# Neighbour keys made on VectorE in bf16, and attention products for two gathers at once with ScalarE copying the sums

## The chip, the cores and the metric

The kernel runs on one core of a Trainium2 chip. The metric is device time in microseconds (us) of one execution, and a kernel's time is the median over several runs. The core's engines run at the same time, each through its own stream of instructions in order: TensorE (PE; its weight loads are listed as PEld), VectorE (DVE), ScalarE (ACT), GpSimd (POOL) and SyncE (SP). Transfers to and from main memory are issued by an engine's queue and run beside it.

## The reference

Two layers over 4096 nodes with 128 features. The graph is a random 0/1 matrix `adj` with density 1/128, so a node has some 32 neighbours (a list has room for 64). Layer 0 is graph attention with eight heads, layer 1 takes three quantiles over the neighbours that a rule keeps.

```python
# layer 0, cut
Wh = jnp.einsum('nd,hde->hne', nodes, W)
f1 = jnp.einsum('hnd,hd->hn', Wh, a1)
f2 = jnp.einsum('hnd,hd->hn', Wh, a2)
e = leaky_relu(f1[:, :, None] + f2[:, None, :], 0.2)
att = softmax(where(adj > 0, e, -9e15))
h = elu(jnp.einsum('hnm,hmd->hnd', att, Wh))
x = elu(cat(h) @ W1 + b1)
x = layernorm(nodes + x, gamma, beta)
# layer 1, cut
svals = sort(where(keep, x[neighbours], big))
agg = mean over q in (0.25, 0.5, 0.75) of svals[ceil(q * n_keep) - 1]
out = (0.5 * agg + 0.5 * x) @ W.T + b + x
```

## The kernel before

No dense attention matrix is made. Each tile of 128 nodes is first searched for the list of its neighbours; then a gather fetches, for each place of the list, the row of that neighbour; and the softmax-weighted sum of the rows is taken before the product with W (the sum over neighbours and the product with W change places).

**Search** (`neighbours`, L535 to L589). The adjacency of a tile comes in two halves of 128x2048 int32, loaded from ScalarE's queue (L544, three buffers). ScalarE makes it `sgn`, 0 or 1 in bf16, and counts it (L550, two buffers). Per piece of 512 columns TensorE makes search keys in PSUM: 8192 times sgn (L571, lhsT `markb`) plus a falling count of columns from `parts` (L573). VectorE takes the eight largest of each 128 columns (L577, four `max8` per piece) into `first`, 128x256. After the second half, eight rounds of `max8` and `match_replace` (L584, L586) give the 64 largest in order, and L589 takes the 8192 off again, so that a list holds falling positions, padded with zeros. `neighbours` yields after each piece and each pair of rounds, so others can be placed between.

**Blocks.** Tiles go in blocks of 2, 8 and 22 (L377 to L417). The nodes of a block are ranked by their number of neighbours (`rank_by_count`) and scattered in that order, so that tile i of a block needs only lists up to a cap, from 24 to 63 places. The first 2 tiles are searched at the start, the next 8 while the first block is attended, the next 22 while the second is. In these two blocks `tc.manual_schedule` keeps the order of the written program on VectorE, TensorE and ScalarE (`ORDERED`, L410). In the last block, with no search left, a scheduler orders the instructions.

**One step** (`step`, L345 to L375) fetches tile i, weighs tile i-1 and transforms an earlier group of tiles. `fetch_rows` (L755 to L813) loads the lists on SP's queue, transposes them (L786) and the scores f1 (L794, L799), and issues the indirect gathers on GpSimd (L185). One gather brings 128 rows: 32 places of the lists of four nodes in a part of width 32, which has 32 gathers for the 128 nodes, or 16, 8 or 4 places of 8, 16 or 32 nodes in parts of that width, which have as many gathers as places. So a tile with cap 35 has parts of 32 and 4 and takes 36 gathers. A part of 32 fills a buffer G, a short rest goes into Gs (16 gathers); both have two buffers, and G a third in the last block. `weigh_rows` (L816 to L901) is cut by yields, between which the step takes a turn of the transform and `each` pieces of the search.

**Weighing.** For each part: z = exp(leaky_relu(f1 + f2)) (L829 and L830 on VectorE, L831 on ScalarE); pf, 128x1024, which spreads z onto the right nodes (L835); then TensorE sums G's rows over the partitions with columns of pf as weights into y (L847), one matmul for each gather, or two or more where its nodes and heads pass 128 columns. The result has a row for each node and head of the gather (4 x 8 = 32 rows in a full part) and 129 columns: 128 features and a one, for the denominator. y is three PSUM banks with one buffer and holds 8 blocks of 128x129. So in a full part four matmuls fill the rows of one block. After the last part VectorE takes the denominators (L868, L875) and normalises out of PSUM (L879). TensorE transposes (L896) and ScalarE copies yT (L897).

**Transform** (`transform`, L904 to L988) does, for two tiles (four in the last block), the products with W (L939, into hT), the exp of the elu (L947), the elu (L917, L919), the product with W1 (L925), a second elu (L952 to L956), and the layer norm (L966 to L986), whose rows a GpSimd scatter writes to x1 (L194, called x_d in the trace). hT comes from the pool `pp` in the first two blocks and from the key pool `kp` in the last.

**Quantiles.** The rest gathers rows of x1 (L185, named vals) and sorts them in a network of minima and maxima on VectorE (L1145), with copies by ScalarE (L1141).

Of the kernel before, what the change touches and what calls it, by code (L numbers as in the profile page):

```python
# [23 lines left out]
H = 8  # L24
# [9 lines left out]
MARK = 8192.0  # L34
# [30 lines left out]
TURN = 12  # L65

# [142 lines left out]
def kernel(  # L209
# [97 lines left out]
    parts = adjp.tile([64, N], BF16, name="parts", bufs=1)  # L307
    markb = adjp.tile([P, P], BF16, name="markb", bufs=1)
    nc.vector.memset(oneb, 1.0)
    nc.vector.tensor_scalar(markb, ident, MARK, None, ALU.mult)  # L310

    nc.gpsimd.memset(parts, 0.0)
    iota(nc, parts[0:1, :], [[-64, N // 64], [0, 64]], base=N)
    iota(nc, parts[32:33, :], [[0, N // 64], [-1, 64]])
# [4 lines left out]
    def search(t0, n):  # L319
        return neighbours(  # L320
            tc, adjp, kp, rec, num, adj, range(t0, t0 + n), parts, markb, oneb
        )
# [22 lines left out]
    def step(fetch=None, pieces=None, quota=0, size=2, more=None):  # L345
# [5 lines left out]
        if len(weigh) > 1 or (weigh and not fetch):  # L351
# [3 lines left out]
            turns = sum(2 + -(-w // 8) for w, *_ in parts) + 3  # L355
# [9 lines left out]
            if len(members) == size:  # L365
                tails.append(
                    transform(tc, attp, pp, more or pp, turned.pop(0), list(members), consts, store)
                )
                members.clear()
# [8 lines left out]
    for b, n in enumerate(BLOCKS):  # L378
# [28 lines left out]
        else:  # L407
            pieces = search(t0 + n, BLOCKS[b + 1])
            quota = -(-BLOCKS[b + 1] * PIECES // n)
            with tc.manual_schedule(engines=ORDERED):  # L410
                for i in range(n):
                    step((recs_d[b], i, CAPS[n][i], t0 + i), pieces, quota)
# [122 lines left out]
def neighbours(tc, adjp, kp, rec, num, adj, tiles, parts, markb, oneb):  # L535
# [24 lines left out]
    while signs:  # L560
# [7 lines left out]
        for b in range(half // 512):  # L568

            key = kp.tile([P, 512], F32, name="key")  # L570
            nc.tensor.matmul(key, lhsT=markb, rhs=sgn[:, ts(b, 512)], start=True, stop=False)  # L571
            c0 = i * half + b * 512
            nc.tensor.matmul(  # L573
                key, lhsT=oneb[0:64, :], rhs=parts[:, c0 : c0 + 512], start=False, stop=True
            )
            for c in range(512 // CW):
                nc.vector.max(first[:, ts(c0 // CW + c, 8)], key[:, ts(c, CW)])  # L577
# [3 lines left out]
        nc.vector.tensor_tensor(num[:, t : t + 1], cnt[:, 0:1], cnt[:, 1:2], ALU.add)  # L581
        for r in range(L // 8):
# [6 lines left out]
        nc.vector.tensor_scalar(rec[:, t, 0:L], rec[:, t, 0:L], -MARK, 0.0, ALU.add, ALU.max)  # L589
# [165 lines left out]
def fetch_rows(tc, ap, narrow, rec_d, i, cap, t, xt_d, bad, turn):  # L755
# [26 lines left out]
    for s0, w in layers(cap):  # L782
# [22 lines left out]
        elif s0 % 32 == 0:  # L805

            few = sum(v for s, v in layers(cap) if s >= s0) <= 16
            G, col = take(ap, [P, 16 if few else 32, XW], "Gs" if few else "G", turn), 0
# [7 lines left out]
def weigh_rows(tc, ap, pools, pp, parts, turned, place, size, consts):  # L816
# [5 lines left out]
    y = pp.tile([P, 3, 512], F32, name="y")  # L822

    def block(b):
        return y[:, b // 3, (b % 3) * (D + 1) : (b % 3 + 1) * (D + 1)]

# [568 lines left out]
```

## The time and the profile before

| what | value |
|---|---|
| median of 6 runs | 4426.52 us (4419.93 to 4429.68) |
| profiled execution | 4424.82 us |
| span of it | 4423.1 us |
| mean granted TensorE clock | 0.558 |
| busy: PE, PEld | 979.5 us (22%), 516.9 us (12%) |
| busy: VectorE | 2532.4 us (57%) |
| busy: ScalarE | 1029.0 us (23%) |
| busy: GpSimd | 2296.4 us (52%) |
| gathers G of attention | 1092, mean 972 ns |

By time, the span falls into: start, with the search of two tiles (0 to 95 us); the first block, with the search of eight (95 to 320); the second block, with the search of 22 (322 to 1110); ranking and scattering (1110 to 1180); the last block (1180 to 2380, with a tail to 2444); the quantiles (2444 to 4423). Each stage has its own busy engine, so the shares over the whole span say little about one of them.

A line of the waits names the engine and line that waited, what released it, and then microseconds in total, number of times and the longest. "remote" is a releaser that can't be named from the records, and "issue" is time in which the engine waited for nothing that the profile shows. In lists of groups, x stands ahead of a count, then come busy microseconds and mean nanoseconds of one, and after the second bar the idle time ahead.

### The profile page before, as it was taken

To read this page: it belongs to the slowest core of one execution; us is meant where nothing else is said; L and a number is where in the kernel's file an instruction comes from. 1 tells how busy PE (TensorE), PEld (TensorE's weight loads), DVE (VectorE), ACT (ScalarE), POOL (GpSimd) and SP (SyncE) were. 2 spreads that over 40 slices of the span, in tenths; PEclk is the share of its full clock that TensorE was granted. 3 is DMA by queue.
4 is the path that set the end of the run, shared out by engine and by line. 5 is a ranking of instruction groups with operands and counts; after the bars stand their busy time and mean duration, and the time that the engine had idled before them with its cause. 6 is when DMAs were issued, how large, how long until landed. Compare 5 with 4: busy or idle time off the path is not lost. (4 is left out here: it accounts for less than half of the span.)

```text
span 4423.1 us, 19775 instructions
## 1 busy us (share of the span) xinstructions
PE 979.5 (22%) x4289; PEld 516.9 (12%) x4289; DVE 2532.4 (57%) x4862; ACT 1029.0 (23%) x1424; POOL 2296.4 (52%) x2453
## 2 busy tenths in 40 slices
PE   4323444443222233233233000000000001000101
PEld 2001211111111111121122000000000000000001
DVE  5554556555321124111121437888878999999898
ACT  2101212111000011000010213333333444434333
POOL 2433443344567666757564675666575334455530
PEclk9955555556556555555565555555555555555555
DMA  5313323221121121212111111111111001111100
GB/s 169 107 48 113 99 91 107 88 93 43 48 49 50 47 56 44 58 41 56 44 49 32 48 52 39 48 45 48 35 50 36 23 21 33 31 36 36 38 28 3
DMA packets 115233, 241.26 MB, mean 55 GB/s; under 512 B 51904, under 2 KB 68288, under 8 KB 106912
## 3 DMA queue, kind: packets, MB, share of 16 engines
q0 software_dynamic: 76224, 161.01, 13.2%
q10 hardware_dynamic: 12160, 68.49, 4.4%
q1 hardware_dynamic: 26720, 10.41, 1.1%
q14 instruction: 93, 0.76, 0.1%
q8 instruction: 36, 0.59, 0.1%
HBM read 228.56 MB, written 11.18 MB: 54 GB/s over the span
## 5 line engine op out<-in xcount | busy, mean ns | idle before, releaser
L1145 DVE TENSOR_TENSOR vals<-low,vals 128x1024 f32<-128x1024 f32 (+9 forms) x1359 | 1402.2, 1057 | 333.6 <-ACT low L1141 116.1
L185 POOL DMA_INDIRECT G<-xt_d,idx x1092 | 1061.0, 972 | 730.5 <-issue 400.2
L185 POOL DMA_INDIRECT vals<-x_d,idx x960 | 911.0, 949 | 296.0 <-issue 283.5
L1141 ACT COPY low<-vals 128x1024 f32<-128x1024 f32 (+10 forms) x701 | 607.2, 876 | 971.6 <-DVE vals L1145 662.7
L1155 PE MATMUL st_ps<-ident,u 128*128 128x128 f32 x344 | 86.2, 433 | 1776.4 <-ACT u L1154 1346.4
L577 DVE MAX8 first<-key 128x8 f32<-128x128 f32 x1024 | 223.7, 283 | 346.4 <-remote 230.7
L194 POOL DMA_INDIRECT out_dram<-o,own_i x32 | 31.8, 993 | 619.9 <-ACT o L1167 617.5
L847 PE MATMUL y<-G,pf 128*32 128x129 f32 (+2 forms) x2224 | 215.1, 397 | 501.4 <-issue 352.8
L1155 PEld LDWEIGHTS st_ps<-ident,u 128*128 128x128 f32 x344 | 75.1, 323 | 1787.4 <-ACT u L1154 1353.6
L571 PE MATMUL key<-sgn,markb 128*128 128x512 bf16 x256 | 148.5, 580 | 531.4 <-DVE first L577 320.2
L868 DVE TENSOR_SCALAR rden<-y 128x6 f32<-128x6 f32 x64 | 7.3, 153 | 380.3 <-PE y L847 229.6
L847 PEld LDWEIGHTS y<-G,pf 128*32 128x32 f32 (+2 forms) x2224 | 141.0, 170 | 576.1 <-issue 411.8
L550 ACT ACTIVATE sgn<-adj_t 128x2048 bf16<-128x2048 int32 x64 | 122.0, 1906 | 358.7 <-PE key L571 178.2
L917 DVE TENSOR_SCALAR e<-e 128x512 f32<-128x512 f32 x64 | 28.1, 439 | 295.5 <-issue 276.5
L897 ACT COPY yT<-turned 128x512 f32<-128x512 f32 x64 | 65.5, 1024 | 550.6 <-PE turned L896 394.8
L925 PE MATMUL o<-hv,W_sb 128*128 128x256 f32 (+1 forms) x176 | 104.6, 712 | 204.1 <-DVE e L917 75.6
L573 PE MATMUL key<-parts,oneb 64*128 64x512 bf16 x256 | 146.9, 574 | 1.1 <-issue 1.0
L194 POOL DMA_INDIRECT x_d<-x,R x32 | 32.9, 1028 | 194.4 <-DVE x L986 162.9
L1145 DVE TENSOR_TENSOR most<-low,most 128x1024 f32<-128x1024 f32 (+7 forms) x116 | 131.8, 1166 | 2.6 <-ACT low L1141 0.5
L185 POOL DMA_INDIRECT Gs<-xt_d,idx x92 | 89.8, 976 | 81.7 <-PE y L847 54.9
L584 DVE MAX8 rec<-first 128x8 f32<-128x256 f32 x256 | 109.2, 427 | 29.0 <-issue 12.5
L831 ACT ACTIVATE z<-z 128x256 f32<-128x256 f32 (+3 forms) x62 | 20.3, 329 | 452.8 <-DVE z L830 421.5
(187 smaller groups left out, 1797.6 us busy)
## 6 DMA issues: line engine op xcount, KB each, us to landing
adj_t<-in_adj_dram ACTq DMA_DIRECT2D x64, 1024.0 KB
G<-xt_d,idx POOLq DMA_INDIRECT x1092
vals<-x_d,idx POOLq DMA_INDIRECT x960
R<-rec_d SPq DMA_DIRECT2D x128, 26.4 KB
xt_d<-rec SPq DMA_DIRECT2D x4, 548.0 KB
score<-rec_d SPq DMA_DIRECT2D x132, 1.0 KB
rec<-in_x_dram SPq DMA_DIRECT2D x4, 512.0 KB
Gs<-xt_d,idx POOLq DMA_INDIRECT x92
```

Source lines behind the costliest of these rows:

```text
L185: nc.gpsimd.indirect_dma_start(out=dst, out_offset=None, in_=rows, in_offset=bass.IndirectOffsetOnAxis(ap=idx, axis=0),)
L550: nc.scalar.activation(sgn, adj_t, AF.Sign, accum_out=cnt[:, i : i + 1])
L571: nc.tensor.matmul(key, lhsT=markb, rhs=sgn[:, ts(b, 512)], start=True, stop=False)
L573: nc.tensor.matmul(key, lhsT=oneb[0:64, :], rhs=parts[:, c0 : c0 + 512], start=False, stop=True)
L577: nc.vector.max(first[:, ts(c0 // CW + c, 8)], key[:, ts(c, CW)])
L584: nc.vector.max(top, first)
L847: nc.tensor.matmul(block(b)[p0 : p0 + m, :], lhsT=pf[:, c : c + m], rhs=G[:, g, 0 : D + 1], start=(i == 0 and b % 3 == 0), stop=last, skip ...
L897: nc.scalar.copy(yT[:, :, ts(place, P)].rearrange("p h (u g) -> p g u h", u=4)[:, ts(half, 16)], t_ps.rearrange("p b (g u h) -> p (b g) u ...
L925: nc.tensor.matmul(o, lhsT=consts["W1_sb"][:, h, :], rhs=hv[:, ts(j, n)], start=(h == 0), stop=(h == H - 1),)
L1141: nc.scalar.copy(kept, low)
L1145: nc.vector.tensor_tensor(high if end else low, kept, high, ALU.max if end else ALU.min)
L1155: nc.tensor.matmul(st_ps, lhsT=u, rhs=ident, start=(i == 0), stop=(i == len(terms) - 1))
```

## The change

**Search.** The keys are made in place: `sgn` times `back`, a row of 128 down to 1, on VectorE in bf16 and SBUF (128x512 a piece, `back` broadcast over four chunks). `max8` then reads these. So a key is a position within its chunk of 128 columns; after the second half two operations of 128x256 add the chunk's offset from a constant `chunk` to keys above zero. `parts`, `markb` and the subtraction at the end go, and the two matmuls a piece with them. The constants are iotas on GpSimd as before.

**Weighing.** z of all parts is made first. Then the tile goes through in two halves, each with a pf of 128x512 per part (five buffers). A half has four blocks of 128 output rows; each lies in a PSUM bank of its own (`YBANKS`, four buffers, of 258 columns), and a matmul covers two gathers: its weights are 64 columns of pf (both gathers' 32), and the moving rows are both gathers' rows side by side, so two quarters of the result are the sums and the other two are not used. For parts of width 8 and 4, and of 16 beside a part of 32, the same rows stand twice. ScalarE copies the used sums to `raw` in SBUF, in pieces of 32x129 (64x129 where the widest part is 16), and VectorE normalises there, in one operation instead of two.

**Around it.** hT always comes from the key pool. The number of turns is counted for the new yields. A buffer Gs has 12 rows instead of 16.

```diff
@@ -304,21 +304,18 @@
     adjp = tc.alloc_tile_pool(name="adjp", bufs=2, side="right")
     cp = tc.alloc_tile_pool(name="cnt", bufs=2, side="right")
     kp = tc.alloc_tile_pool(name="key_ps", bufs=2, space=PSUM)
-    parts = adjp.tile([64, N], BF16, name="parts", bufs=1)
-    markb = adjp.tile([P, P], BF16, name="markb", bufs=1)
+    back = adjp.tile([P, CW], BF16, name="back", bufs=1)
+    iota(nc, back, [[-1, CW]], base=CW)
+    chunk = adjp.tile([P, NCH, 8], F32, name="chunk", bufs=1)
+    iota(nc, chunk, [[-CW, NCH], [0, 8]], base=N - CW)
     nc.vector.memset(oneb, 1.0)
-    nc.vector.tensor_scalar(markb, ident, MARK, None, ALU.mult)
-
-    nc.gpsimd.memset(parts, 0.0)
-    iota(nc, parts[0:1, :], [[-64, N // 64], [0, 64]], base=N)
-    iota(nc, parts[32:33, :], [[0, N // 64], [-1, 64]])
     rowi = adjp.tile([P, P], F32, name="rowi", bufs=1)
     iota(nc, rowi, [[1, P]])
     nc.vector.tensor_scalar(before, rowi, pidx, None, ALU.is_gt)
 
     def search(t0, n):
         return neighbours(
-            tc, adjp, kp, rec, num, adj, range(t0, t0 + n), parts, markb, oneb
+            tc, adjp, rec, num, adj, range(t0, t0 + n), back, chunk
         )
 
     for _ in search(0, BLOCKS[0]):
...
@@ -352,7 +349,7 @@
             R, parts = weigh.pop(0)
             place = len(members)
             members.append(R)
-            turns = sum(2 + -(-w // 8) for w, *_ in parts) + 3
+            turns = len(parts) + 13
             each = -(-quota // turns)
             done = 0
             for _ in weigh_rows(tc, attp, pools, pp, parts, turned, place, size, consts):
...
@@ -364,7 +361,7 @@
             quota -= done
             if len(members) == size:
                 tails.append(
-                    transform(tc, attp, pp, more or pp, turned.pop(0), list(members), consts, store)
+                    transform(tc, attp, pp, more, turned.pop(0), list(members), consts, store)
                 )
                 members.clear()
         elif not fetch:
...
@@ -409,7 +406,7 @@
             quota = -(-BLOCKS[b + 1] * PIECES // n)
             with tc.manual_schedule(engines=ORDERED):
                 for i in range(n):
-                    step((recs_d[b], i, CAPS[n][i], t0 + i), pieces, quota)
+                    step((recs_d[b], i, CAPS[n][i], t0 + i), pieces, quota, more=kp)
                 for _ in pieces:
                     pass
         t0 += n
...
@@ -567,18 +564,22 @@
             first = adjp.tile([P, NCH * 8], F32, name="first")
         for b in range(half // 512):
 
-            key = kp.tile([P, 512], F32, name="key")
-            nc.tensor.matmul(key, lhsT=markb, rhs=sgn[:, ts(b, 512)], start=True, stop=False)
+            key = sgn[:, ts(b, 512)].rearrange("p (c w) -> p c w", w=CW)
+            nc.vector.tensor_tensor(
+                key, key, back.unsqueeze(1).to_broadcast([P, 512 // CW, CW]), ALU.mult
+            )
             c0 = i * half + b * 512
-            nc.tensor.matmul(
-                key, lhsT=oneb[0:64, :], rhs=parts[:, c0 : c0 + 512], start=False, stop=True
-            )
             for c in range(512 // CW):
-                nc.vector.max(first[:, ts(c0 // CW + c, 8)], key[:, ts(c, CW)])
+                nc.vector.max(first[:, ts(c0 // CW + c, 8)], key[:, c, :])
             yield
         if i == 0:
             continue
         nc.vector.tensor_tensor(num[:, t : t + 1], cnt[:, 0:1], cnt[:, 1:2], ALU.add)
+        above = adjp.tile([P, NCH * 8], F32, name="above", bufs=1)
+        nc.vector.scalar_tensor_tensor(
+            above, first, 0.0, chunk.rearrange("p c k -> p (c k)"), ALU.is_gt, ALU.mult
+        )
+        nc.vector.scalar_tensor_tensor(first, first, 0.0, above, ALU.max, ALU.add)
         for r in range(L // 8):
             top = rec[:, t, ts(r, 8)]
             nc.vector.max(top, first)
@@ -586,7 +587,6 @@
                 nc.vector.match_replace(first, top, first, 0.0)
             if r % 2:
                 yield
-        nc.vector.tensor_scalar(rec[:, t, 0:L], rec[:, t, 0:L], -MARK, 0.0, ALU.add, ALU.max)
 
 
 def complete_records(tc, cp, rec, num_all, bad, jp1, pidx, t0, n):
@@ -804,8 +804,8 @@
             G, col = take(ap, [P, 32, XW], "G", turn), 0
         elif s0 % 32 == 0:
 
-            few = sum(v for s, v in layers(cap) if s >= s0) <= 16
-            G, col = take(ap, [P, 16 if few else 32, XW], "Gs" if few else "G", turn), 0
+            few = sum(v for s, v in layers(cap) if s >= s0) <= 12
+            G, col = take(ap, [P, 12 if few else 32, XW], "Gs" if few else "G", turn), 0
         for g in range(w):
             gather(nc, G[:, col + g, :], xt_d, idx[:, g : g + 1])
         parts.append((w, k, G[:, col : col + w, :], f1v))
@@ -819,72 +819,63 @@
     nc = tc.nc
     own, ident = consts["own"], consts["ident"]
 
+    zs = []
+    for w, k, G, f1v in parts:
+        z = ap.tile([P, 32, H], F32, name="z", bufs=4)[:, 0:w, :]
         nc.vector.tensor_tensor(z, G[:, :, D + 1 :], f1v, ALU.add)
         nc.vector.scalar_tensor_tensor(z, z, ALPHA, z, ALU.mult, ALU.max)
         nc.scalar.activation(z, z, AF.Exp)
+        zs.append(z)
         yield
+
+    split = 2 if parts[0][0] == 32 else 1
+    raw = ap.tile([P, H, D + 1], F32, name="raw", bufs=1)
+    for half in range(2):
+        pfs = []
+        for (w, k, G, _), z in zip(parts, zs):
+            g2 = w // 2
+            pf = ap.tile([P, H * P // 2], F32, name="pf", bufs=5)
+            spread = [P, g2, k, H]
+            nc.vector.tensor_tensor(
+                pf.rearrange("p (g k h) -> p g k h", g=g2, k=k),
+                z[:, ts(half, g2), :].unsqueeze(2).to_broadcast(spread),
+                own[w].unsqueeze(1).unsqueeze(3).to_broadcast(spread),
+                ALU.mult,
+            )
+            pfs.append(pf)
         yield
+        for b in range(4):
+            y = pp.tile([P, 512], F32, name="y", bufs=YBANKS)[:, 0 : 2 * (D + 1)]
+            yv = y.rearrange("p (a d) -> p a d", a=2)
+            for i, ((w, k, G, _), pf) in enumerate(zip(parts, pfs)):
+                both = w == 32 or (w == 16 and split == 1)
+                m = max(min(k * H, P) * (2 if both else 1), 32)
+                for p0 in range(0, P, m):
+                    c = b * P + p0
+                    g = half * (w // 2) + c // (k * H)
+                    if both:
+                        rhs = G[:, g : g + 2, 0 : D + 1]
+                    else:
+                        rhs = G[:, g : g + 1, 0 : D + 1].to_broadcast([P, 2, D + 1])
+                    nc.tensor.matmul(
+                        yv[p0 : p0 + m],
+                        lhsT=pf[:, c : c + m],
+                        rhs=rhs,
+                        start=(i == 0),
+                        stop=(i == len(parts) - 1),
+                        skip_group_check=True,
+                    )
+            m = P // (2 * split)
+            for p0 in range(0, P, m):
+                a = p0 // m % 2
+                nc.scalar.copy(raw[p0 : p0 + m, 4 * half + b, :], yv[p0 : p0 + m, a, :])
+            yield
 
     rden = ap.tile([P, H], F32, name="rden")
+    nc.vector.tensor_scalar(rden, raw[:, :, D], TINY, None, ALU.max)
     nc.vector.reciprocal(rden, rden)
+    yn = raw[:, :, 0:D]
+    nc.vector.tensor_tensor(yn, yn, rden.unsqueeze(2).to_broadcast([P, H, D]), ALU.mult)
     yield
     if place == 0:
         wide = [P, H, size * P]
...
@@ -930,10 +921,7 @@
                     stop=(h == H - 1),
                 )
         if k < steps:
-            if more is pp:
-                hT = pp.tile([P, 512], F32, name="hT")[:, 0 : hp * n]
-            else:
-                hT = more.tile([P, 512], F32, name="key")[:, 0 : hp * n]
+            hT = more.tile([P, 512], F32, name="key")[:, 0 : hp * n]
             for j in range(hp):
                 h = k * hp + j
                 nc.tensor.matmul(
```

In `weigh_rows` the removed lines are left out of the diff; they are L824 to L887 of the listing above.

More of the change, by code (lines that the diff above doesn't have):

```diff
@@ L33 @@
 NCH = N // CW
-MARK = 8192.0
 PIECES = N // 512 + L // 16
@@ L65 @@
 TURN = 12
+YBANKS = 4
 R_NUM, R_OWN, R_F1 = L, L + 1, L + 2
@@ L532, in node_rows, with neighbours @@
     nc.sync.dma_start(xt_d[N:, :], pad)
-def neighbours(tc, adjp, kp, rec, num, adj, tiles, parts, markb, oneb):
+def neighbours(tc, adjp, rec, num, adj, tiles, back, chunk):
     nc = tc.nc
@@ L820, in weigh_rows @@
     own, ident = consts["own"], consts["ident"]
-    y = pp.tile([P, 3, 512], F32, name="y")
-    def block(b):
-        return y[:, b // 3, (b % 3) * (D + 1) : (b % 3 + 1) * (D + 1)]
-    for i, (w, k, G, f1v) in enumerate(parts):
-        z = ap.tile([P, 32, H], F32, name="z")[:, 0:w, :]
+    zs = []
+    for w, k, G, f1v in parts:
+        z = ap.tile([P, 32, H], F32, name="z", bufs=4)[:, 0:w, :]
         nc.vector.tensor_tensor(z, G[:, :, D + 1 :], f1v, ALU.add)
@@ L831, in weigh_rows @@
         nc.scalar.activation(z, z, AF.Exp)
+        zs.append(z)
         yield
-        pf = ap.tile([P, H * P], F32, name="pf")
-        spread = [P, w, k, H]
-        nc.vector.tensor_tensor(
-            pf.rearrange("p (g k h) -> p g k h", g=w, k=k),
-            z.unsqueeze(2).to_broadcast(spread),
-            own[w].unsqueeze(1).unsqueeze(3).to_broadcast(spread),
-            ALU.mult,
-        )
-        yield
-        last = i == len(parts) - 1
-        m = min(k * H, P)
-        for g in range(w):
-            for c in range(g * k * H, (g + 1) * k * H, m):
-                b, p0 = c // P, c % P
-                nc.tensor.matmul(
-                    block(b)[p0 : p0 + m, :],
-                    lhsT=pf[:, c : c + m],
-                    rhs=G[:, g, 0 : D + 1],
-                    start=(i == 0 and b % 3 == 0),
-                    stop=last,
-                    skip_group_check=True,
-                )
-            if g % 8 == 7 or g == w - 1:
-                yield
@@ L858, in weigh_rows @@
-    rden = ap.tile([P, H], F32, name="rden")
-    yn = ap.tile([P, H, P], F32, name="yn", bufs=1)
-    spans = ((0, 2, 6), (2, 1, 2))
-    views = []
-    for bank, banks, n in spans:
-        c = n // banks
-        views.append(
-            y[:, bank : bank + banks, 0 : c * (D + 1)].rearrange("p a (c d) -> p a c d", c=c)
-        )
-    for (bank, banks, n), v in zip(spans, views):
-        nc.vector.tensor_scalar(
-            rden[:, 3 * bank : 3 * bank + n].rearrange("p (a c) -> p a c", a=banks),
-            v[:, :, :, D],
-            TINY,
-            None,
-            ALU.max,
-        )
@@ L875, in weigh_rows @@
-    nc.vector.reciprocal(rden, rden)
-    for (bank, banks, n), v in zip(spans, views):
-        here = slice(3 * bank, 3 * bank + n)
-        c = n // banks
-        nc.vector.tensor_tensor(
-            yn[:, here, :].rearrange("p (a c) d -> p a c d", a=banks),
-            v[:, :, :, 0:D],
-            rden[:, here]
-            .rearrange("p (a c) -> p a c", a=banks)
-            .unsqueeze(3)
-            .to_broadcast([P, banks, c, D]),
-            ALU.mult,
-        )
+    split = 2 if parts[0][0] == 32 else 1
```

## The prediction, made before the changed kernel ran

> **What bounds the kernel now.** I read the page's first two parts, then busy time by stage, then the waits of each stage. The profiled execution took 4424.8 us with a span of 4423.1; the median of the six runs shown is 4426.5, so a saving in the span carries over one to one.
>
> ```profile
> DVE  5554556555321124111121437888878999999898
> POOL 2433443344567666757564675666575334455530
> ```
>
> Each digit is one of 40 slices of 110.6 us. From slice 23 on (2444 us) VectorE is the limit in the quantile stage, which the change does not touch. Before it three stages count: the first two blocks with the search between (95 to 320, 322 to 1110), where nothing is above six tenths, and the last block (1180 to 2380), where GpSimd gathers at 0.6 to 0.7. Busy time by stage, columns PE, PEld, DVE, ACT, POOL:
>
> ```profile
> 95.00:320.00 225.00, 78.41 (x215) 20.47 (x216) 130.22 (x518) 30.51 (x32) 94.66 (x100) 0.75 0.28 88
> 322.00:1110.00 788.00, 318.24 (x1327) 130.06 (x1326) 422.98 (x1569) 128.91 (x152) 314.04 (x324) 0.56 0.28 89
> 1180.00:2380.00 1200.00, 349.35 (x1808) 193.53 (x1809) 241.64 (x630) 93.69 (x140) 790.79 (x809) 0.57 0.20 50
> ```
>
> In the middle stage VectorE, the busiest, is idle for 365 of 788 us. The waits of that window say for what:
>
> ```profile
> PE key L571 <- DVE first L577: 229.2, 33, 35.0
> DVE first L577 <- remote: 203.9, 20, 31.3
> ACT sgn L550 <- PE key L571: 96.1, 12, 39.7
> DVE first L577 <- PE key L573: 68.0, 65, 9.7
> ```
>
> The search's maxima (L577) wait 204 us for a releaser that the profile can't name and 68 us for TensorE's key; so VectorE stands behind TensorE. The largest such wait ends at 830 us, and nothing of TensorE is recorded from 801.6 to 830. Why TensorE stands still is seen in the last block, in its own rows:
>
> ```profile
> 1826.03 0.37 PE L847 MATMUL y<-G,pf 128*32 128x129 f32 x1 [2.43 <-issue]
> ...
> 1833.73 0.38 PE L847 MATMUL y<-G,pf 128*32 128x129 f32 x1 [2.42 <-issue]
> ```
>
> A row of 0.37 us every 2.1 to 2.8 us, waiting for nothing shown, though the gathered data are there (z was made of them). Elsewhere 64 such records pass in 3.67 us. The starts differ by multiples of 0.70 us, and an f32 matmul has four issued instructions, 4 x 0.70 = 2.80: TensorE's stream trickles at about 0.70 us per instruction. These stretches come once for each packet of instruction queue q8 (36 in the span). I read them as cost per TensorE instruction, whatever it computes. The last block pays too, where GpSimd waits for the sums to free G (window 1180 to 2430):
>
> ```profile
> POOL Gs L185 <- PE y L847: 54.9, 4, 23.1
> POOL G L185 <- PE y L847: 42.0, 2, 26.8
> POOL G L185 <- DVE f1b L794: 35.4, 3, 15.8
> ```
>
> **The change part by part.** Counting f32 matmuls as four instructions and bf16 as two, the built kernels issue to TensorE: first block 446 before, 134 after; middle stage 2798 and 1326; last block 4566 and 3350.
>
> *Keys.* The 512 bf16 matmuls of L571/L573 go. For each of 256 pieces VectorE gains a bf16 product of 128x512, for each of 32 tiles two 128x256 operations, and loses L589 (195 ns). Durations:
>
> ```profile
> L677 DVE TENSOR_TENSOR u<-u 128x448 bf16<-128x448 bf16 x1 | 0.4, 382 | 0.0
> L664 DVE TENSOR_TENSOR hot<-jp,capped 128x512 bf16<-128x512 f32 x1 | 0.7, 679 | 0.0
> L830 DVE SCALAR_TENSOR_TENSOR z<-z 128x256 f32<-128x256 f32 x24 | 10.1, 421 | 0.5
> ```
>
> From the first, plus the slope to L677's 128x896 (609 ns), 512 cost 0.38 + 64 x 0.51 ns = 0.41 us; the second is the upper end, if the broadcast operand or writing in place loses the fast rate. I take 0.41, the same types. A maximum now reads bf16 SBUF instead of f32 PSUM: bounds zero gain and the 283 ns a row costs; I take no change. Middle stage: 176 x 0.41 + 22 x (2 x 0.42 - 0.20) = 72 + 14 = +86 us VectorE (upper end 176 x 0.68 + 14 = 134). First block: 64 x 0.41 + 8 x 0.64 = +31. Two 3.85-us iotas and a 3.5-us memset of POOL become two smaller iotas at the start, 0 to -10 us, hidden by the adjacency loads: 0. The start's own 16 pieces gain 8 us of VectorE under the same loads (DVE 49 of 95): 0, at worst +8.
>
> *Weighing.* 1240 sum matmuls become 728, of 258 columns. Per full 32-gather part TensorE did 64 records in 3.7 us, four column groups at once; two groups with twice the columns are about 8 us by the same rows, and small parts double as well, half of their columns being copies: some +9 us per tile. In 31 tiles it lies under 35 gathers of 1.25 us (0.94 + 0.30 issue) = 44 us; on the last it is bare. pf is the same elements in two calls (one 1217 ns, two f32 128x512 at about 0.68 each): +0.15 us per part. rden and yn read SBUF and lose a call; yn's rows 951 + 413 ns become one: nothing either way. ScalarE gets 928 copies of 129 columns; the 128x128 copies out of PSUM take 262 to 267 ns (L1160, L510): 32 x 0.26 = 8.4 us per tile, 67 in the middle stage on 129 busy of 788. That is hidden by idle time, but ScalarE runs in order: behind a copy waiting for a slow sum stand the next Sign (L550), whose tiles feed the search, and exp (L947), for which TensorE's next products wait. Two sgn buffers put four pieces, about 5 us, between. So the search is detached from TensorE only partly.
>
> *Buffers.* G is released only after a tile's second half instead of part by part, and the next use waits on that. y alternates over four banks of one ring. SP's loads and x1's scatter on POOL keep their order; hT moves to the key ring, which now serves it alone.
>
> *Sums by stage.* Middle: of the waits, 68 us for keys vanish; the 204 us shrink with TensorE's instructions, 204 x 1326/2798 = 97, saving 107; +86 come. If none of the new VectorE work finds cover: -68 - 107 + 86 = -89. If all of it lies in the remaining 190 us of idle time: -175. Bound above, if the stalls stay at 204 through ScalarE and products run at the slow rate: -68 + 134 = +66. I take -130, halfway in the first two, as the search's pieces are interleaved with idle gaps of the same steps. First block: waits there 26.8 and 28.5 (whole-window 230.7 and 96.5 less the middle's), of which 19 + 28 go, +31 come: -16 to -47, I take -30. Last block: of 97 us waiting for y, instructions down 27% give -26; all gone gives -97; G held longer, up to another 97, is the bad end. I take -50. Tail after the last gather (2380 to 2444): +9 of TensorE, 8 of copies, against 27% fewer instructions: +10, bounds 0 and +20. Sum -30 - 130 - 50 + 10 = -200: 4424.8 - 200, about **4225 us**.
>
> A rule against it: the Trainium skill, "SBUF — State Buffer", section "SBUF: two separate sides", says that VectorE operations with two SBUF inputs or in a two-port mode can lock GpSimd out of a shared port, so that gathers starve for descriptors. This trace disagrees: in the quantile stage, with VectorE busy nine tenths on two-input products, gathers take 949 ns (L185, 960 of vals), against 972 of G beside an idler VectorE. By the rule, an estimate, each of 240 products would cost a gather up to its own 0.41 us, about +100; I add nothing.
>
> **The rivals.**
> A. *Slower: release of G becomes the limit.* One mechanism: a tile's gathers can't reuse G until its second half has gone through, and that half runs at the trickle. 152 instructions per tile (3350/22) x 0.70 = 107 us, if wholly in a trickle, against 44 us of gathers. For it: the seven waits for y above. Against: two buffers, a third in the last block, and 57 fewer instructions. If the waits for y double (+97), the tail costs 20 and the same held chain leaves the middle stage at its upper end and the first block at -16 (+66 - 16), the time is 4425 + 167 = 4592; with the first two stages at nothing and the y waits up by half, 4425 + 49 + 20 = 4494. I name 4510 for it. It decides from the point where the last block loses what the first two gain less the tail, 30 + 130 - 10 = 150: y waits of about 97 + 150 = 247 us.
> B. *Only the search gains.* GpSimd's waits in the last block stay 156 us (the y waits move to f1b and x): -160 + 10: 4275.
> C. *No change.* ScalarE's in-order copies pass TensorE's stalls on to the signs (for it: 96 us of Sign already wait for L571), so the stalls stay whole: -68 + 86 + 10 of the tail - 26 in the last block = +2: 4427.
> D. *All stalls go:* -47 - 175 - 97 + 0: 4105.
>
> **Chances.** Main 0.40, B 0.20, D 0.10, C 0.08, A 0.22. A difference of 0.2% (9 us) is about what a measurement of this kernel can tell. Faster is main, B and D: 0.70; same 0.08; slower 0.22. The likeliest case's terms, all at their ends but without the upper bounds, run from 4106 to 4314; halfway to each is its own range, 4165 to 4270. The full range is 4105 to 4460: it takes in D, C and the near third of A, leaving some 0.16 above and 0.04 below.
>
> **What would show it.** Right: no L577 wait on PE; about 0.41 us a product; middle stage near 658 us; last block's y waits under 70 us; quantile stage still about 1980 us long. Wrong: products at 0.68; Sign or exp waiting long for ScalarE's own copies; G or Gs waiting over 97 us for y; TensorE rows of the sums 0.7 us apart per instruction as often as before.

## The result, and the profile after

The changed kernel took 4433.44 us (median of 18 runs) against 4427.05 of the kernel before (39 runs): the ratio is 1.0014 with a 95% interval of 1.0005 to 1.0024. It is slower by a hair, where 4225 us was forecast. In a later batch, on a chip where the kernel before takes 4455 us, the ratio was 1.0025 (1.0016 to 1.0035).

One thing has to be known to read the times below. The runs came in batches from several chips, and these are of two kinds. In four batches the kernel before took 4427, 4427, 4455 and 4437 us, in three others 3835, 3837 and 3836; only ratios to the kernel before on the same chip are compared, and stages only between chips of one kind. The traces of the first kind have the trickle, the stretches of the prediction in which an engine gets an instruction only every 0.70 us or a multiple of it; those of the second have not, as the two probes show. The kernel before was profiled on a chip of the first kind only.

Stages, cut at GpSimd's first scatter of each block's records and at its first gather of the quantiles (profiled executions, us):

| stage | before | after | forecast of the difference |
|---|---|---|---|
| start | 77.7 | 77.0 | 0 |
| first block | 244.2 | 243.0 | -30 |
| second block with the search of 22 tiles | 788.4 | 765.7 | -130 |
| ranking and last block, to the last gather | 1268.0 | 1294.5 | -50 |
| tail | 66.1 | 79.0 | +10 |
| quantiles | 1978.7 | 1977.6 | 0 |

The second part of the page after, of which the same two rows were shown of before:

```profile
DVE  5665667757120215111112527888878999999898
POOL 2432343454757465756573675666575334455530
```

VectorE is fuller than before in slices 2 to 8 and in slice 10 (by one tenth, in slices 8 and 10 by two), and the quantile stage begins in the same slice. Busy time by stage, columns as shown of before, for the second block and from the ranking to the quantiles:

```profile
319.99:1085.73 765.74, 181.68 (x595) 101.10 (x596) 505.79 (x1785) 192.03 (x393) 319.52 (x324) 0.57 0.29 92
1085.73:2459.26 1373.53, 442.58 (x1464) 221.48 (x1462) 282.82 (x734) 277.47 (x820) 825.95 (x854) 0.62 0.18 46
```

In the second block VectorE is busy for 506 us, 82 more than before, and idle for 260, 105 less: 82 - 105 = -23 is the whole of what that stage gained. Its waits there:

```profile
DVE first L573 <- remote: 79.8, 19, 6.5
DVE z L825 <- DMA G<-xt_d,idx: 37.3, 4, 21.2
DVE bad L776 <- DMA R<-rec_d: 25.3, 1, 25.3
DVE rec L585 <- remote: 17.4, 9, 3.0
```

No maximum waits for TensorE any more (68 us before), and the nameless wait of the maxima fell from 204 to 80. But L585 (17.4 us, 1.8 for the same operation before) now waits for what VectorE itself has just made, and so does L573: the first maximum of each piece waits for one semaphore, that of its product. The waits of GpSimd from 1180 to 2460:

```profile
POOL G L185 <- issue: 238.8, 677, 16.2
POOL x_d L194 <- DVE x L974: 109.4, 4, 39.1
POOL Gs L185 <- remote: 28.7, 3, 15.9
POOL Gs L185 <- PE y L860: 28.1, 2, 17.7
POOL G L185 <- PE y L860: 27.3, 2, 15.0
```

The named waits for y are 55 us in place of 97, with some 44 more that have no name (11 before). New is a wait of 39 us of x1's scatter for the first four tiles of that block, which stands behind 217 of the block's gathers in GpSimd's queue, where it stood behind 249. New too are three gathers that start late, by 16.2, 9.2 and 8.0 us, with nothing shown that they wait for; the longest of these gaps before was 0.4 us.

### The profile page after: what moved, and what is told of

It reads as the page before. It is cut to its first block, busy times and chain, and to the rows that moved or that the text cites. A ratio compares the mean times of both kernels' runs of the same rounds, so it can differ in the third digit from the quotient of the medians.

```text
span 4436.9 us, 18414 instructions
## 1 busy us (share of the span) xinstructions
PE 811.0 (18%) x2753; PEld 467.8 (11%) x2753; DVE 2633.7 (59%) x5147; ACT 1264.5 (28%) x2352; POOL 2281.6 (51%) x2452
## 5 line engine op out<-in xcount | busy, mean ns | idle before, releaser
L871 ACT COPY raw<-y 32x129 f32<-32x129 f32 (+1 forms) x928 | 239.1, 258 | 848.1 <-remote 559.6
L860 PE MATMUL y<-G,pf 128*64 128x258 f32 (+1 forms) x1200 | 286.6, 517 | 935.0 <-issue 478.2
L573 DVE MAX8 first<-sgn 128x8 f32<-128x128 bf16 x1024 | 223.7, 280 | 138.3 <-remote 115.8
L860 PEld LDWEIGHTS y<-G,pf 128*64 128x64 f32 (+1 forms) x1200 | 141.7, 191 | 1064.7 <-issue 753.1
L839 DVE TENSOR_TENSOR pf<-z,own 128x512 f32<-128x512 f32 x124 | 80.4, 681 | 110.2 <-issue 82.5
L887 PE MATMUL turned<-ident,raw 128*128 128x128 f32 x256 | 68.7, 421 | 402.6 <-DVE raw L878 250.2
L585 DVE MAX8 rec<-first 128x8 f32<-128x256 f32 x256 | 109.2, 427 | 36.2 <-remote 24.3
```

The source lines that it names most:

```text
L573: nc.vector.max(first[:, ts(c0 // CW + c, 8)], key[:, c, :])
L585: nc.vector.max(top, first)
L839: nc.vector.tensor_tensor(pf.rearrange("p (g k h) -> p g k h", g=g2, k=k), z[:, ts(half, g2), :].unsqueeze(2).to_broadcast(spread), own[w] ...
L860: nc.tensor.matmul(yv[p0 : p0 + m], lhsT=pf[:, c : c + m], rhs=rhs, start=(i == 0), stop=(i == len(parts) - 1), skip_group_check=True,)
L871: nc.scalar.copy(raw[p0 : p0 + m, 4 * half + b, :], yv[p0 : p0 + m, a, :])
L887: nc.tensor.transpose(t_ps[:, b, :], yn[:, 4 * half + b, :], ident)
```

## The experiments

**Which half of the change does what.** search_only puts the change's `neighbours` and its constants into the kernel before; weigh_only puts the old search back into the changed kernel.

```diff
# search_only, against before
-            nc.tensor.matmul(key, lhsT=markb, rhs=sgn[:, ts(b, 512)], start=True, stop=False)
+            nc.vector.tensor_tensor(key, key, back.unsqueeze(1).to_broadcast([P, 4, CW]), ALU.mult)
# weigh_only, against after: the reverse of it
```

> The kernel before with the change's search alone (keys by VectorE in bf16; the weighing as it was). Handshake theory (in stretches of gathers each wait that an engine must see acknowledged comes in steps of 0.70 us, on every engine, so the count of waits matters and not of instructions): the first two stages keep the 25 us that the changed kernel gained there and the last block stays at 1334 us, so 4400 to 4410. Instruction theory (0.70 us per TensorE instruction): the sums still issue 4960 instructions, but 1024 of the keys go, all in the first two stages: 4380 to 4400. ScalarE theory (its copies hold the signs and cost the expected gain): without the copies the stage gains the forecast 130, so about 4300.

> The changed kernel with the search of before (keys by TensorE in PSUM). Handshake theory: the last block keeps the 40 us that it lost, and the middle stage loses the waits that the search by VectorE had saved: 4450 to 4480. Instruction theory: fewer sums' instructions, so faster than before: 4380 to 4410. ScalarE theory: copies hold the signs as in the changed kernel, and TensorE's keys come on top: 4450 to 4500, with ScalarE's raw copies named ahead of Sign.

search_only: 4406.6 against 4426.5, ratio 0.9957 (0.9943 to 0.9970). weigh_only: 4471.5, ratio 1.0106 (1.0092 to 1.0120). Both lie where the handshake theory had them. The search alone gains 20 us and the weighing alone loses 45; together they lose 6 and not 25. weigh_only issues some 1600 fewer instructions on TensorE than the kernel before (512 sums less at four each, 467 more that only wait) and is slower: the forecast that the time follows the number of TensorE's instructions falls here.

**Fewer waits on TensorE.** before_reversed takes the gathers of a part from last to first, so that only 440 of the matmuls carry a wait in place of 1184.

```diff
-        for g in range(w):
+        for u, g in enumerate(reversed(range(w))):
-                    start=(i == 0 and b % 3 == 0),
+                    start=(i == 0 and b in (2, 5, 7)),
```

> The kernel before, with the sums of a part taken from its last gather to its first. The same matmuls, but TensorE meets the latest gather of each queue first, so that 440 of them carry a wait instead of 1184. Handshake theory: the trickle of L847 goes, the last block gains 30 to 80 us and the middle stage up to 20: 4330 to 4400. Instruction theory: same instructions, same trickle, 4427 within 9 us. A loss is possible only where a sum now waits for its part's last gather, which z has waited for before.

4422.6, ratio 0.9991 (0.9981 to 1.0000), and the stages are those of before to 2 us. Waits for gathers that landed long before cost TensorE nothing.

**The trickle by itself.** probe adds stretches of small operations behind the last output.

```diff
+            for j in range(80):
+                gather(nc, here[:, j, :], xt_d, own_i[:, j % NT : j % NT + 1])
+                for j in range(300):
+                    nc.scalar.copy(pc[:, j, :], pa)
```

> The kernel before, with seven stretches of small work added behind the last output, six of them beside 80 gathers (100 us). Handshake theory: a ScalarE-VectorE handoff costs some 0.5 us alone and 1.4 us or more beside gathers; 300 independent ScalarE or VectorE copies go at full speed beside gathers (0.17 and 0.1 us each); a chain of VectorE operations that wait for each other slows to 0.7 us or more each; 80 TensorE matmuls without waits stay under 0.4 us each, with a wait each for data long landed they take 2 to 3 us. Instruction theory: the independent copies and the matmuls without waits slow to 0.7 us per instruction as well.

Timeline of ScalarE in probe, beside gathers that were issued from 4572.0 to 4670.6 (start, length, what, count, idle before):

```profile
4570.10 1.68 ACT L504 COPY pc<-pa 128x16 f32<-128x16 f32 x15
4573.61 0.20 ACT L504 COPY pc<-pa 128x16 f32<-128x16 f32 x1 [1.83 <-issue]
4575.01 0.20 ACT L504 COPY pc<-pa 128x16 f32<-128x16 f32 x1 [1.20 <-issue]
...
4691.21 0.20 ACT L504 COPY pc<-pa 128x16 f32<-128x16 f32 x1 [0.39 <-issue]
4691.91 20.36 ACT L504 COPY pc<-pa 128x16 f32<-128x16 f32 x192 [0.49 <-issue]
```

Fifteen copies that wait for nothing run at 0.11 us each, ahead of the first gather; from then on most come 0.70 or 1.40 apart, until 21 us after the last gather's issue, when the other 192 run at full speed. VectorE ran 94 independent copies, most of them beside the first gathers, before it fell within some 15 us to seven per 10 us, and TensorE's rows, two to a matmul, after 82 and 89 at full speed, came mostly 2.1 to 2.8 apart with a wait or without. So the handshake theory can't be the whole of the trickle, which takes instructions that wait for nothing as well. That the kernels lose time at waits all the same is shown in the section on the prediction.

probe_two (three engines at once, and long products) came to a chip of the other kind:

> Four stretches behind the last output, each beside 80 gathers: 200 independent ScalarE copies; the same with 200 VectorE copies; the same with 100 TensorE matmuls as well; 90 VectorE products of 128x1408 (about 1.5 us each). A supply for each engine: 1.4 us per copy in all three of the first, on each engine. One supply for all: 2.8 us with two engines, 5 us or more with three. The long products run without gaps in either case, since each lasts longer than the supply takes. On a chip without the trickle everything runs at full speed.

```profile
3853.16 21.21 ACT L503 COPY pc<-pa 128x16 f32<-128x16 f32 x200
```

The 200 copies run without a gap, 19 us of them beside gathers, and so did VectorE's and TensorE's work and the 90 long products. No trickle is seen on that chip, and the kernel before takes 13% less on those of its kind. Whether the supply is one for each engine or one for all stays open, as do the long products beside the trickle.

**ScalarE's copies.** copies_doubled makes each copy in two; bank_copies makes one of a whole bank in place of four and lets VectorE pick the quarters; copies_shared gives half of those of the last block to VectorE.

```diff
# copies_doubled
+                for c0, c1 in ((0, 65), (65, D + 1)):
+                    nc.scalar.copy(raw[p0 : p0 + m, 4 * half + b, c0:c1], yv[p0 : p0 + m, a, c0:c1])
# bank_copies
+            nc.scalar.copy(raw[:, 4 * half + b], yv)
# copies_shared
+                copy = nc.vector.tensor_copy if a and len(pools) > 1 else nc.scalar.copy
```

> The changed kernel with each of ScalarE's 928 copies made in two (65 and 64 columns): the same elements, the same waits, 928 more ScalarE instructions, some 640 of them in the last block. Supply theory (beside gathers an engine gets a new instruction only every 1.4 us on ScalarE or VectorE and four in 2.8 us on TensorE, whatever they do): if a fifth to a half of the 640 lie in such stretches and on the chain, 640 x 1.4 x 0.2 to 0.5 = 180 to 450 us more, 4610 to 4880. Handoff theory (the cost is in the round trip from TensorE to ScalarE and back): the same round trips, 4430 to 4460.

> The changed kernel with one ScalarE copy of a whole bank (128x258, half of it not needed) in place of four of 32x129: 256 copies instead of 928, and six more VectorE operations per tile, which pick the quarters. The same round trips between TensorE and ScalarE. Supply theory: the last block gets 40 to 150 us shorter than in the changed kernel, the middle stage 0 to 20: 4270 to 4395, so faster than before. Handoff theory: 4430 within 15.

> The changed kernel with half of the copies of the last block on VectorE, which is idle there. Supply theory with a supply for each engine: the two halves trickle side by side, 30 to 100 us less, 4330 to 4400. Supply theory with one supply for all engines: 4430 within 15. Handoff theory: one more engine in each round trip, 4430 to 4470.

All three came to a chip without the trickle: ratios 1.0077, 1.0129 and 1.0059 (intervals within 0.0016). The first two were run again on one with it, beside the changed kernel; copies_shared was not:

> The changed kernel itself, beside the kernel before on the same chip. The last four runs came from a chip where the kernel before takes 3835 us and no trickle is in the traces, the ones ahead from one where it takes 4427 with the trickle; which one comes now shows in the time of before. Supply theory: with the trickle 4433 again; without it the last block is bound by the gathers (1155 to 1163 us in all four) and only the middle stage counts, where one copy more or less should not matter: within 10 us of copies_doubled, ratio 1.004 to 1.008. If the forecast's sum of the search (VectorE's new work finding cover) held without the trickle, the ratio would be under 0.99.

> As copies_doubled. On a chip with the trickle: supply theory 100 us or more above the changed kernel, over 4530; handoff theory 4430 to 4460. On a chip without it: 1.008 again.

> As bank_copies. On a chip with the trickle: supply theory 20 to 150 us less than the changed kernel, 4280 to 4413; handoff theory 4433 within 15. On a chip without it: 1.013 again.

after_again 1.0025, copies_doubled_2 1.0063 (1.0042 to 1.0084), bank_copies_2 1.0091 (1.0056 to 1.0127). ScalarE's instructions in the last block went from 820 to 1476 and to 349, and that block's time, with ranking and tail, from 1386 to 1396 and to 1381. Supply theory asked for 100 us or more in the one and a gain of at least 20 in the other: the number of copies is not what the block lost. The timelines of a stretch show it too. First the changed kernel, then bank_copies_2:

```profile
1602.76 1.07 ACT L871 COPY raw<-y 32x129 f32<-32x129 f32 x4 [10.73 <-remote]
1613.21 1.07 ACT L871 COPY raw<-y 32x129 f32<-32x129 f32 x4 [9.38 <-remote]
1624.41 1.06 ACT L871 COPY raw<-y 32x129 f32<-32x129 f32 x4 [10.13 <-remote]
```

```profile
1608.43 0.38 ACT L869 COPY raw<-y 128x258 f32<-128x258 f32 x1 [10.83 <-remote]
1619.63 0.37 ACT L869 COPY raw<-y 128x258 f32<-128x258 f32 x1 [10.82 <-remote]
1630.83 0.38 ACT L869 COPY raw<-y 128x258 f32<-128x258 f32 x1 [10.83 <-remote]
```

Four copies or one, a bank passes every 10 to 11 us in such stretches (outside them most follow in under 10); 11.20 is sixteen steps of 0.70. So the pitch there belongs to the bank and not to its copies. A bank takes some three matmuls and, in the trace, further TensorE instructions that only wait (402 of them for the last block's 512 sums, against 41 for 816 before); that they come from a matmul over two gathers having two to wait for is argued. Where the 11 us go can be read from the trace's records of semaphores, the counters that an instruction raises when it is done and another waits for:

```profile
1603.89 1.20 PE L860 MATMUL y<-G,pf 128*64 128x258 f32 x4 [7.29 <-issue]
1614.33 1.20 PE L860 MATMUL y<-G,pf 128*64 128x258 f32 x4 [9.24 <-issue]
```

The changed kernel's rows of one bank end at 1605.1. TensorE's semaphore is raised at 1608.99 and again at 1613.18, 4 and 8 us later; ScalarE's four copies start at 1613.21, and the next bank's rows 0.05 us after these end. So of the 10.44 us from bank to bank some 8 are signals that come late for work that is done.

**The product's size.** search_wide is search_only with one product for half a row; after_wide is the same edit on the changed kernel; wide_plus_idle adds 192 writes of one column where products were saved.

```diff
-            nc.vector.tensor_tensor(key, key, back..., ALU.mult)          # 128x512, four times
+            if b == 0:
+                nc.vector.tensor_tensor(keys, keys, back..., ALU.mult)    # 128x2048, once
+            else:
+                nc.vector.memset(idle[:, n : n + 1], 0.0)                 # wide_plus_idle alone
```

> The kernel before with the change's search, the product made once for half a row of the adjacency (128x2048) instead of four times 128x512: 192 VectorE instructions fewer than search_only, 132 of them in the middle stage. Supply theory: a third to all of the 132 at 1.4 us, 60 to 180 less at most, and at least the arithmetic: 4340 to 4395. If only the arithmetic counts (176 x 0.41 less 44 x 1.2 = 19 us, in part hidden): 4388 to 4407.

> As search_wide. On a chip with the trickle: supply theory 4340 to 4395; arithmetic alone 4388 to 4407. On a chip without it: 1.001 again.

> The changed kernel with the product made once for 128x2048 instead of four times 128x512: 192 VectorE instructions fewer. If VectorE's supply of instructions beside gathers holds the middle stage, it gains what search_wide_2 gained over search_only, 72 us, and the time is 60 to 90 us below the changed kernel, ratio 0.984 to 0.990 to before. If the weighing holds it instead (ScalarE's copies ahead of the signs), under 25 us less. On a chip without the trickle: within 15 us of the changed kernel.

> search_wide with 192 writes of one column each added on VectorE, without waits, in the places of the products that it saved: the instruction count of search_only (5702 against 5705), none of its arithmetic and none of its added waits. Supply theory: back to search_only, middle stage 750 to 775 and ratio 0.993 to 0.998. If the products' arithmetic or their waits were the cost: stays at search_wide_2, middle stage about 700 and ratio 0.975 to 0.980.

> As wide_plus_idle. On a chip with the trickle (before at 4427 to 4455 us): supply theory, back to search_only, middle stage 750 to 775, ratio 0.993 to 0.998; if the products' arithmetic or waits were the cost, middle stage about 700, ratio 0.975 to 0.980. On a chip without it: 1.001 again.

Without the trickle: search_wide 1.0011, wide_plus_idle 1.0013, after_wide 0.9990 (0.9981 to 1.0000). after_wide did not come to a chip with it, so what its edit is worth there stays open; on one chip without it, the second block takes 588 us in after_wide and 612 in late_scatter (below), which has the four products. With it: search_wide_2 4342.1 against 4455.2, ratio 0.9745 (0.9720 to 0.9770), and wide_plus_idle_2 0.9712 (0.9688 to 0.9736). The second block took 767 us in search_only, 696 in search_wide_2 and 686 in wide_plus_idle_2, on three chips (the changed kernel took 766 and 772 there on two chips). The 132 idle instructions of that block (7.8 us) cost nothing, so the supply theory, as a count of instructions on VectorE, falls for this stage too. The groups of that stage, first of search_only, then of search_wide_2:

```profile
L573 DVE MAX8 first<-sgn 128x8 f32<-128x128 bf16 x704 | 153.6, 280 | 55.5 <-remote 37.2 <-issue 13.1
L568 DVE TENSOR_TENSOR sgn<-sgn,back 128x512 bf16<-128x512 bf16 x176 | 71.9, 409 | 8.9 <-ACT sgn L547 8.9
```

```profile
L574 DVE MAX8 first<-sgn 128x8 f32<-128x128 bf16 x704 | 144.7, 278 | 37.6 <-remote 22.2 <-issue 12.3 <-DVE sgn L569 2.0
L569 DVE TENSOR_TENSOR sgn<-sgn,back 128x2048 bf16<-128x2048 bf16 x44 | 53.2, 1209 | 10.4 <-ACT sgn L547 8.9 <-issue 1.5
```

VectorE's busy time there fell by 19 us (497 to 478) and its idle time by 53 (270 to 217). The wide product also has one wait for VectorE's own result where four were, 44 in place of 176. By the semaphore that each wait of over 0.5 us was for, VectorE waited in that stage for its own signals 104 us in search_only (45 waits), 75 in search_wide_2 (28) and 60 in wide_plus_idle_2 (30), and for ScalarE's 90, 50 and 48 us; search_wide, without the trickle, has no such wait for an own signal. These two kinds fell by 69 us from search_only to search_wide_2, and other idle time grew by 16. Why the waits for ScalarE fell was not isolated. Of the versions tried on both kinds of chip search_wide is the one to keep: faster than both kernels on the chips with the trickle, level with the kernel before on the others.

**The early scatter.** late_scatter holds x1's rows back for one step in the last block.

```diff
+        while held:
+            scatter(nc, x1_d, *held.pop(0))
+        held.extend(store)
```

> The changed kernel with x1's scatter issued one step later in the last block, where the order of GpSimd's queue puts it at the places that it has in the kernel before. Queue theory: the wait of 39 to 44 us for the layer norm in the first scatter of the last block goes, the last block is 25 to 45 us shorter, ratio 0.993 to 0.998 to before. If the wait only moves to the gathers behind (TensorE's and ScalarE's work being late in any case), the time stays within 10 us of the changed kernel, 1.0025.

> As late_scatter. On a chip with the trickle: queue theory, the last block 25 to 45 us shorter than the 1374 to 1386 of the changed kernel and ratio 0.993 to 0.998; if the wait only moves to the gathers behind it, 1.000 to 1.005 and the last block within 10 us of the changed kernel's. On a chip without it: 1.009 again.

Both came to chips without the trickle (1.0091 and 1.0082), so whether the 39 us of that wait would go stays open.

## Why the prediction was wrong

Right were the prices on VectorE: a product took 409 ns (0.41 forecast), the operations of 128x256 took 424 and 423, half a pf 681 (0.68), ScalarE's copies 257 (0.26), and the second block's VectorE grew by 82 us (86 forecast). The bf16 maxima in SBUF cost 280 ns against 283. The key waits went (68), the nameless wait of the second block's maxima shrank by 124 (107 forecast), the tail grew by 13 (10 forecast), and the quantile stage stood still. Right too was to add nothing for gathers held up by these products: in the trace after, gathers that overlap a product of 128x512 took 0.99 us on average, the others 0.97. A longer product does show: in search_wide_2 the 67 gathers that overlap one of 128x2048 took 1.20 us, the others 0.98.

The time of 4433 us lies in the full range, 4105 to 4460, which was made wide to take in the rivals, and outside the main account's own, 4165 to 4270. Wrong was the step that turned the prices into time, in three places.

*"I read them as cost per TensorE instruction, whatever it computes."* The nameless wait of 204 us was rightly laid on TensorE, but not on the number of its instructions. The key for the wait that ends at 830 was done at 801.6, and TensorE then waited for VectorE:

```profile
801.23 0.39 PE L573 MATMUL key<-parts,oneb 64*128 64x512 bf16 x1
823.01 0.60 ACT L947 ACTIVATE e<-hT 128x512 f32<-128x512 f32 x1 [26.90 <-remote]
830.00 0.89 DVE L577 MAX8 first<-key 128x8 f32<-128x128 f32 x4 [31.31 <-remote]
830.95 0.61 PE L571 MATMUL key<-sgn,markb 128*128 128x512 bf16 x1 [29.33 <-DVE first L577]
```

Both the exp and the maxima wait for TensorE's semaphore. The trace has it raised at 822.99, 826.48 and 829.98, in steps of 3.5 us (five times 0.70), and each of the two starts 0.02 us after one of these. So TensorE's work was done, and the signal of it came up to 28 us later. Such waits go when VectorE has nothing of TensorE's to wait for, and not when TensorE has fewer instructions. By the semaphore that each wait of over 0.5 us was for, VectorE waited for TensorE in the second block 268 us before (44 waits), 232 us in weigh_only (65 waits), which has some 1600 fewer TensorE instructions in all and takes 45 us more, and not at all in the changed kernel. Nor is 0.70 us the price of a TensorE instruction in a stretch: a row of the trace is half of an f32 matmul (2480 rows for 1240 sums), two of the four instructions, so rows 2.80 us apart are 1.40 us each, as many of the probe's copies were. And not each packet of queue q8 brings a stretch: search_wide and search_wide_2 both have 32 such packets, and only the second ran with the trickle.

*The cover, "-130, halfway in the first two, as the search's pieces are interleaved with idle gaps".* This is the step that lost the forecast gain: VectorE's waits for its own new work were put at nothing. A maximum has to wait until its product is signalled as done, and on VectorE too this signal comes late:

```profile
439.93 0.40 DVE L568 TENSOR_TENSOR sgn<-sgn,back 128x512 bf16<-128x512 bf16 x1
445.44 0.87 DVE L573 MAX8 first<-sgn 128x8 f32<-128x128 bf16 x4 [5.10 <-remote]
```

The product ends at 440.33, VectorE's semaphore is raised at 445.41, and the maximum starts at 445.44. Such waits for own signals take 158 us of the second block (53 waits over 0.5 us), 95 of them at the maxima; before they took 3 us (2 waits). So waits for TensorE's late signals were changed for waits for VectorE's own: -268 + 155 + 82 = -31, where the stage gained 23; the other waits make up the 8. That these waits belong to the trickle and not to the program is shown by late_scatter_2 and copies_shared, which do the same in that block on chips without it: 612 and 613 us in place of 766, VectorE busy for 506 us as here, and not one wait of over 0.5 us for an own signal. The first block went the same way: 50 us of waits for TensorE's signals went, those for own signals grew from 29 to 58, VectorE is busy for 27 us more, and the stage is 1 us shorter where 30 was forecast.

*The last block, "instructions down 27% give -26".* The count left out the TensorE instructions that only wait, 62 before and 403 after in that block, and took a transpose as four instructions where the traces show two: 4212 against 3328, 21% less and not 27. (The counts of the second block are too high in the same way: 2653 and 1191 in the traces for 2798 and 1326.) And even that drop did not show: GpSimd's waits for y, named and nameless, went from 108 us to 100. What came in is the scatter's wait of 39 us and the 33 us ahead of three gathers; 33 us of waits for f1b, turned and rden went. The loss needs the trickle: on chips without it, this block with ranking and tail takes 1155 to 1165 us with the new weighing and 1162 to 1163 with the old; on chips with it 1368 to 1386 and 1334 to 1353. Late signals are part of it, some 8 us of a bank's 10.44 in a stretch, but how the whole loss adds up is not shown. Argued from the timelines is the order: z of all parts is made first, and then, in a stretch, a bank passes from TensorE to ScalarE every 11 us, where the sums of a first part ran beside the gathers of the next before. No run undid that alone. Nor do the halves of the change add up here: to the last gather, search_only takes 18 us more than before, with the old weighing, weigh_only 23, and both together 26.

Of the rivals, "only the search gains" has the right signs, at a size of 20 us for the search and with a loss in the weighing that it did not have. "Release of G becomes the limit" (its 57 fewer instructions a tile are 55 by the prediction's own counts) asked for doubled waits for y, which did not come. "No change" was nearest in time; its mechanism, ScalarE's copies holding the signs, is not borne out: search_only has none of these copies, and its second block takes 767 us against the changed kernel's 766. Nor did doubling or quartering them move that stage as it asks (776 and 795 against 772 us, the latter with VectorE busy for 30 us more).

## What to carry to other kernels

Idle time next to a stall is not free room. Before new work is costed at nothing under it, count the waits that come with it, those of an engine for its own last operation too: here the maxima waited 95 us for products that took 72 us to make. When an engine waits for something without a name, look whether its input was already there, and when the semaphore that it waits for was raised; if that is long after the input was made, a leaner producer gains little, and what there is to gain lies in fewer waits. Making four products one took the search from a ratio of 0.9957 to 0.9745 on chips with the trickle, while 132 idle instructions that wait for nothing cost nothing there. Merging the sums of another engine two by two took 512 matmuls away and brought 467 instructions that only wait; it cost 45 us with the old search.

## What was not expected of the hardware

The same program runs at 4427 to 4455 us on some chips and at 3835 to 3837 on others. On the slower ones ScalarE, VectorE and TensorE fall, beside a burst of gathers, to about one instruction in 0.70 to 1.40 us: in the probe ScalarE at once, VectorE after 94 copies at full speed, and they stay so for 21 and 13 us after the last gather is issued. The difference is idle time and not slower operations: in the quantile stage, 1979 us in the kernel before against 1825 in search_wide on a chip without the trickle, VectorE is busy for 1639 us in both. In the kernels it shows at the signals between instructions: on the slower chips, in the cases shown, VectorE's own came 5.1 us after the operation's end and TensorE's 28 us, where in late_scatter_2 and copies_shared, on the others, no wait of VectorE for its own signal reached 0.5 us in the second block. What holds the engines and their signals was not found. Every time here is of an execution from which the profiler's records were taken, so that no run tells whether the recording has a part in it.
